# Values' bias moved into VectorE's evacuation of the shared block product, GpSimd's second bias pass dropped, and all places of the order replaced

## The chip, the core and the metric

The kernel runs on one core of a Trainium2 chip. The metric is the device time of one execution in microseconds (us); lower is better. TensorE is called PE below, its weight loads PEld, VectorE DVE, ScalarE ACT, GpSimd POOL and SyncE, which issues the DMAs, SP.

## The reference

64 independent graphs of 256 nodes with 256 features pass through two layers. All arithmetic is float32.

```
# layer 0, for each graph
q, k = x @ Wq + bq, x @ Wk + bk              # 8 heads of 32
attn = softmax(q k^T / sqrt(32))
out  = sum over r in 0..3 of (attn * (adj == r)) @ (x @ Wv[r] + bv[r])
x    = ln(x + out @ Wo + bo);  x = ln(x + gelu(x @ W1 + b1) @ W2 + b2)
# layer 1: two graph attentions, then a feed-forward
h = gat(gat(x, W1, a1), W2, a2)              # leaky relu, mask adj > 0, softmax
h = ln(x + h);  out = ln(h + relu(h @ w_ff1 + b_ff1) @ w_ff2 + b_ff2)
```

The part that is changed is `x @ Wv[r] + bv[r]`, the values of the four relations.

## The kernel before

**Tiling.** A graph fills 128 partitions twice: 256 nodes are two chunks (`C = 2`), 256 features two chunks (`KD = 2`). The values of a graph are a 256 x 256 by 256 x 1024 product, cut into 2 x 2 blocks. It is done in Strassen's manner with seven block products instead of eight: `v_product` (L504 to L511) makes product i, 128 x 512, in a PSUM buffer `v_ps`, and the sums that build the four blocks are made while the products are taken out of PSUM. Product 1 belongs to all four blocks: `v_first` (L522) copies it on ACT into block (0,0) of `v`, and `v_sum` (L518) adds the others on DVE, seven adds a graph, each from one block to the same or another one: block (1,0), for instance, starts as block (0,1) plus product 7. Then `v_bias` (L525) adds the bias rows on POOL: operation `vb1` adds the row of m = 1 to block (1,0), 512 columns, before (1,1) is made from it, and `vb0` adds the row of m = 0 to both blocks of m = 0, 1024 columns.

**Heads.** Of each graph's 2 x 4 heads, `scores` (L531) makes the scores of four heads by matmuls that use 32 rows of the array each, then come maximum, exponential, reciprocal and normalisation (`max`, `exp`, `rec`, `nrm`), a transposition by 32 x 32 squares on DVE with a write to DRAM and a read back (`eT`, `eW`, `eR`), a copy to PSUM (`ec`) and the products with the masks of the relations (`pm` on DVE, `pl` on POOL). `heads_out` (L580, matmuls L589) makes `po` by matmuls that use 32 columns of the array each. Operations `wo`, `st1` to `ln1` finish the attention; `a...` is the first feed-forward (`aT`, `aW`, `aR` transpose its input, `au` are its first products, `ad` its second), `ga...`, `z...`, `h1`, `h2` the graph attentions, `b...` the last feed-forward. The letter-and-number names are keys of `PLACES`.

**Order.** Nothing is scheduled by a compiler. `PLACES` (L28) gives each of a graph's operations a place; graph g's operations stand at `g * PERIOD + place` with `PERIOD = 60`, all are sorted (L781), and each engine carries out its own in that order, strictly one behind the other. The places are not times: a period takes 53.57 us on the chip. So in the steady state each engine repeats one cycle of operations, ordered by place modulo 60, that belong to about seven graphs. The four preparations of weights (`v_weights`, `ffn_weights` twice, `gat_weights`) and the loads of weights have places of their own (L68, L69) and are done once.

**Buffers.** All of PE's products apart from scores and the feed-forward's `po` bank share one PSUM pool of two buffers (`mm_tile`, L121). A product so waits until the reader of an earlier product, usually the last but one, is done.

Of the kernel before, what the change touches and what calls it, by code (L numbers as in the profile page):

```python
# [14 lines left out]
ALU = mybir.AluOpType  # L15
AX = mybir.AxisListType

P = 128
# [7 lines left out]

PERIOD = 60.0
PLACES = {  # L28
    "load": 51.115, "cast": 61.829, "xT": 85.66, "jT": 95.244, "mask0": 96.779, "qk0": 96.964,
    "qkc0": 97.949, "s0": 114.109, "mask1": 114.874, "max02": 120.516, "max01": 124.15, "exp02": 124.943,  # L30
    "rec02": 126.88, "nrm02": 128.516, "max00": 137.875, "max03": 138.248, "exp01": 142.049, "xS": 142.083,
    "eT02": 142.989, "exp00": 144.909, "rec01": 145.054, "qk1": 145.647, "exp03": 145.994, "eW02": 148.03,
    "rec00": 148.295, "qkc1": 149.435, "rec03": 149.477, "nrm01": 152.334, "mask2": 153.228, "vp1": 153.403,
    "nrm00": 154.4, "eT00": 155.05, "vc1": 155.594, "s1": 155.923, "nrm03": 158.066, "max10": 158.616,
    "max11": 159.127, "vp6": 159.308, "y": 159.875, "eR02": 161.643, "max13": 162.676, "mask3": 162.803,
    "exp10": 163.51, "exp13": 164.265, "va6": 164.378, "eW00": 164.574, "vp7": 165.766, "max12": 166.896,
    "vp2": 167.32, "eT03": 167.321, "exp12": 167.329, "va7": 168.263, "va1": 168.656, "pl02": 168.829,
    "eT01": 170.084, "vp5": 171.47, "vb1": 171.744, "va9": 173.956, "exp11": 174.017, "va5": 174.086,
    "eW01": 174.237, "vp4": 174.322, "rec11": 174.688, "rec10": 175.037, "ec02": 175.434, "nrm10": 175.847,
    "va4": 177.865, "nrm11": 178.881, "eW03": 179.53, "eT11": 180.637, "rec12": 181.004, "eR01": 181.498,  # L40
    "rec13": 182.146, "pm02": 182.221, "vp3": 182.341, "nrm13": 182.509, "eR00": 182.73, "mask4": 182.957,
    "ec01": 183.686, "va3": 183.974, "pl00": 184.596, "pm01": 184.674, "nrm12": 185.397, "eT13": 185.431,
    "eR03": 186.516, "ec00": 187.545, "eW11": 189.732, "eW13": 192.489, "pm00": 192.506, "eR11": 192.805,
    "pl03": 192.932, "pl01": 194.193, "ec03": 194.796, "vb0": 194.872, "pm03": 195.848, "eT10": 196.442,
    "eR13": 197.184, "eT12": 197.655, "po0": 199.032, "ec11": 199.429, "eW10": 200.338, "oT0": 203.052,
    "eW12": 203.488, "eR10": 203.542, "pm11": 203.833, "ec13": 205.99, "pm13": 207.559, "pl11": 208.544,
    "ec10": 209.569, "pm10": 210.783, "eR12": 211.055, "pl13": 211.531, "pl10": 212.738, "yb": 213.806,
    "ec12": 214.966, "pm12": 215.614, "pl12": 216.323, "po1": 224.021, "oT1": 226.193, "wo": 231.792,
    "ya": 235.114, "st1": 235.515, "rt1": 236.411, "nb1": 237.487, "ln1": 240.106, "aT": 241.237,
    "aW": 243.237, "aR": 244.635, "au0": 248.422, "au1": 248.889, "ax0": 249.225, "ax1": 250.028,  # L50
    "au2": 253.377, "aS1": 255.511, "ax2": 257.28, "au3": 257.297, "ag": 259.726, "ax3": 259.931,
    "ar": 263.256, "aS3": 265.084, "aS2": 265.188, "aS4": 266.76, "ad1": 267.736, "ad7": 268.061,
    "ad2": 269.978, "ad3": 270.34, "ad4": 270.945, "ae": 271.281, "ad5": 273.751, "ae1": 274.652,
    "ae7": 275.033, "ad6": 277.637, "ae5": 279.375, "ae6": 281.724, "st2": 283.997, "rt2": 284.29,
    "nb2": 285.905, "ln2": 291.498, "lg2": 293.887, "lb2": 294.79, "hT": 297.683, "hW": 300.513,
    "hR": 303.071, "ga0": 304.63, "gac0": 305.433, "ga1": 305.656, "gac1": 307.317, "ipA": 307.666,
    "zA": 307.902, "zmA": 307.921, "zxA": 308.379, "zeA": 312.657, "zdA": 315.675, "h10": 324.462,
    "h11": 325.343, "h1c0": 325.47, "h1c1": 325.478, "ipB": 327.18, "zB": 327.348, "zmB": 328.529,
    "zxB": 330.271, "zeB": 332.506, "zdB": 332.513, "h2": 335.643, "h2a": 335.996, "st3": 338.835,
    "rt3": 339.209, "nb3": 342.44, "ln3": 344.153, "bT": 344.795, "bW": 353.039, "bR": 353.733,  # L60
    "bu0": 358.326, "bu1": 358.559, "bx0": 358.988, "bu2": 361.425, "bx1": 361.898, "bx2": 361.904,
    "bu3": 362.148, "bx3": 363.223, "bS1": 363.277, "bd1": 364.353, "bg": 366.001, "bS2": 366.044,
    "br": 366.414, "bd5": 366.625, "bS4": 368.189, "bd6": 369.237, "bd2": 371.158, "bd3": 371.454,
    "be1": 372.63, "be5": 372.632, "bd4": 372.862, "bS3": 372.912, "be6": 374.175, "be": 375.364,
    "bd7": 377.598, "be7": 378.628, "st4": 383.514, "rt4": 389.43, "nb4": 404.438, "ln4": 418.122,
    "lg4": 419.704, "lb4": 422.082, "store": 423.961,
}
LOAD_PLACE, LOAD_STEP = 96.0, 3.0  # L68
V_PLACE, FFA_PLACE, GAT_PLACE, FFB_PLACE = 100.0, 240.0, 290.0, 300.0  # L69

# [11 lines left out]
def kernel(  # L84
# [12 lines left out]
    nc = tc.nc  # L97
    B, N, D = x.shape
    R = Wv.shape[0]
# [5 lines left out]
    C = N // P  # L105
# [35 lines left out]
    def weight(w, name, mixed=False):  # L141

        k, n = w.shape[0] // P, w.shape[1]
        t = const.tile([P, k, n], F32, name=name)
        if mixed:
            mixed_rows(t, w)
        else:
            loads.append((t, w.rearrange("(k p) n -> p k n", p=P)))
        return t
# [13 lines left out]
    def rowvec(v, n, name):  # L163
        t = const.tile([P, n], F32, name=name)
        loads.append((t, _row(v, n)))
        return t
# [21 lines left out]
    bv_r = const.tile([P, KD, R, P], F32, name="bv_r")  # L188
# [15 lines left out]
    wo, bo_r = weight(Wo, "wo"), rowvec(bo, D, "bo_r")  # L204
# [44 lines left out]
    def seven_weights(b, t):  # L249


        nc.vector.tensor_tensor(t[0], b[0][1], b[1][1], ALU.add)
        nc.vector.tensor_tensor(t[1], t[0], b[0][0], ALU.subtract)
        nc.vector.tensor_tensor(t[2], b[1][0], t[1], ALU.subtract)
        nc.vector.tensor_tensor(b[0][1], b[0][0], b[0][1], ALU.subtract)
        return {1: b[0][0], 2: b[1][0], 3: t[2], 4: b[1][1], 5: t[0], 6: t[1], 7: b[0][1]}

    def v_weights():
        wv_s.update(seven_weights([[wv[:, k, m].rearrange("p r n -> p (r n)") for m in range(KD)] for k in range(KD)],
                                  [wv_t[:, i] for i in range(3)]))  # L260

# [170 lines left out]
    class Graph:  # L432
# [87 lines left out]
            nc.vector.tensor_tensor(self.v_part(*to), self.v_part(*src), self.ps["v", i], ALU.add)  # L520

        def v_first(self):  # L522
            nc.scalar.copy(self.v_part(0, 0), self.ps["v", 1])

        def v_bias(self, m, jcs):  # L525
            v = self.v[m][:, jcs]
            row = bv_r[:, m].rearrange("p r n -> p (r n)")[:, None, :]
            nc.gpsimd.tensor_tensor(v.rearrange("p c r n -> p c (r n)"), v.rearrange("p c r n -> p c (r n)"),  # L528
                                    row.to_broadcast([P, len(range(C)[jcs]), R * P]), ALU.add)

        def scores(self, m):  # L531

# [154 lines left out]
        def operations(self):  # L687

            g, ops = self.g, {}
# [8 lines left out]
            for i in range(1, 8):  # L698
                ops[f"vp{i}"] = lambda i=i: self.v_product(i)

            ops["vc1"] = self.v_first
            for n, to, src, i in (("1", (0, 0), (0, 0), 2), ("6", (0, 1), (0, 0), 6), ("7", (1, 0), (0, 1), 7),
                                  ("5", (1, 1), (1, 0), 5), ("4", (1, 0), (1, 0), 4), ("9", (0, 1), (0, 1), 5),
                                  ("3", (0, 1), (0, 1), 3)):
                ops[f"va{n}"] = lambda to=to, src=src, i=i: self.v_sum(to, src, i)
            ops["vb1"] = lambda: self.v_bias(1, slice(0, 1))
            ops["vb0"] = lambda: self.v_bias(0, slice(0, C))
            for r in range(R + 1):
                ops[f"mask{r}"] = lambda r=r: self.mask(r)
            for m in range(KD):  # L710
# [59 lines left out]
    for place, f in (  # L770
            (V_PLACE, v_weights),
            (GAT_PLACE, gat_weights),
            (FFA_PLACE, lambda: ffn_weights(w1, b1_c, g1_c, be1_c, b2_r, be1_r, "ffa", w2, w2_t)),
            (FFB_PLACE, lambda: ffn_weights(f1, bf1_c, gl1_c, bl1_c, bf2_r, bl1_r, "ffb", f2, f2_t))):
        plan.append((place, len(PLACES), f))
    for g in range(B):
        ops = Graph(g).operations()
# [34 lines left out]
```

## Time and profile before

| what | value |
|---|---|
| median of 3 runs | 3575.66 us (3571.31 to 3575.95) |
| profiled execution, its own time | 3572.94 us |
| its span, first to last instruction | 3571.2 us |
| busy: PE, DVE, ACT, POOL | 3477.1, 2805.2, 2776.8, 3117.9 us |
| mean granted TensorE clock | 0.985 |
| HBM traffic over the span | 125 GB/s |

A busy share is an average over a fill (the first graphs), a long steady state and a drain (the last graphs). The profile's chain of waits follows the work that ended last back through the engines; a piece of PE in it with more microseconds than the same piece elsewhere holds a small pause. A list of waits names the engine that sat idle, the line it then ran, and who ended the wait.

### The profile page before, as it was taken

The numbers are of one execution on the slowest core, as the hardware profiler recorded it, in microseconds if no ns is written. First come the engines' busy times: TensorE is split into PE (matmuls) and PEld (weight loads), VectorE is DVE, ScalarE is ACT, GpSimd is POOL, SyncE is SP. The second block draws the span as 40 slices with busy tenths as digits, with TensorE's granted clock in tenths as the row PEclk, the third lists the DMA queues.
The fourth block names the chain that finished last, engine by engine and source line by source line (L and its number), as shares of the span: only waits on it lengthen the run. The fifth ranks groups of instructions, "written<-read, shape, count | busy, mean of one in ns | idle before, by whom it ended". The sixth has DMA issues, their size and how long they took to land.

```text
span 3571.2 us, 73514 instructions
## 1 busy us (share of the span) xinstructions
PE 3477.1 (97%) x25816; PEld 2704.2 (76%) x25816; DVE 2805.2 (79%) x4952; ACT 2776.8 (78%) x7107; POOL 3117.9 (87%) x3398
## 2 busy tenths in 40 slices
PE   6899999999999999999999999999999999999995
PEld 3677877877877877877877877877877877877875
DVE  5788888888888888788788888888788788788762
ACT  4677877877877877877877877877877877877863
POOL 4688988988988988988988988988988988988974
PEclk8899999999999999999999999999999999999997
DMA  7344444444444444444444444444444444444420
GB/s 198 112 126 127 131 135 127 131 135 127 131 135 127 131 135 128 131 135 126 132 135 125 133 135 125 133 135 122 135 136 122 135 136 122 135 136 123 132 86 27
DMA packets 809890, 457.97 MB, mean 128 GB/s; under 512 B 334256, under 2 KB 718896, under 8 KB 809520
## 3 DMA queue, kind: packets, MB, share of 16 engines
q1 hardware_dynamic: 809520, 453.27, 43.2%
q8 instruction: 203, 3.33, 0.4%
q14 instruction: 167, 1.37, 0.1%
HBM read 243.42 MB, written 201.33 MB: 125 GB/s over the span
## 4 chain that ended last, share of the span: by engine, by line
PE 95%; DMA 1%; DVE 1%; SPq 1%; POOL 1%; ACT 0%; issue 0%; POOLq 0%; ACTq 0%; DVEq 0%
PE po L589 13%; PE ffa_ps L387 12%; PE ffb_ps L387 12%; PE v_ps L511 11%; PE qk_ps L487 6%; PE ffa_po L422 6%; PE ffb_po L422 6%; PE ffa_pq L422 5%; PE ffb_pq L422 5%; PE s L537 4%; PE h_ps L664 3%; PE h_ps L678 3%; PE ga_wps L619 3%; PE wo_ps L609 3%; SPq L139 1%; PE ga_ips L631 0%
## 5 line engine op out<-in xcount | busy, mean ns | idle before, releaser
L572 DVE TENSOR_TENSOR pm<-rel,pe 128x1536 f32<-128x1536 uint8 x512 | 890.9, 1740 | 131.9 <-ACT pe L568 85.3
L577 POOL TENSOR_TENSOR pl<-rell,eT 128x512 f32<-128x512 bf16 x512 | 592.1, 1168 | 29.0 <-DMA eT<-eT_d 24.2
L550 ACT ACTIVATE e<-s,nmax 128x256 f32<-128x256 f32 x1024 | 474.7, 471 | 73.2 <-DVE eT_sq L306 63.6
L387 PE MATMUL ffb_ps<-ffb_T,f 128*128 128x256 f32 x2048 | 458.4, 382 | 24.0 <-DMA ffb_T<-ffb_T_d 23.8
L387 PE MATMUL ffa_ps<-ffa_T,w 128*128 128x256 f32 x2048 | 465.9, 381 | 8.3 <-DMA ffa_T<-ffa_T_d 8.2
L387 PEld LDWEIGHTS ffb_ps<-ffb_T,f 128*128 128x128 f32 x2048 | 392.6, 192 | 106.1 <-issue 39.4
L560 ACT ACTIVATE e<-e,rden 128x256 f32<-128x256 f32 x1024 | 462.4, 506 | 10.3 <-DVE rden L555 10.1
L479 POOL TENSOR_SCALAR rel<-adT 128x512 uint8<-128x512 bf16 x192 | 288.6, 1503 | 198.1 <-DVE pm L572 181.1
L387 PEld LDWEIGHTS ffa_ps<-ffa_T,w 128*128 128x128 f32 x2048 | 381.3, 191 | 57.8 <-ACT e L560 9.6
L520 DVE TENSOR_TENSOR v<-v,v_ps 128x512 f32<-128x512 f32 x448 | 296.0, 672 | 148.2 <-PE v_ps L511 142.5
L589 PE MATMUL po<-pm,v 128*32 128x256 f32 x6144 | 361.6, 384 | 15.7 <-POOL v L528 12.3
L306 DVE STREAM_TRANSPOSE eT_sq<-e 128x512 f32<-128x512 f32 x512 | 350.6, 694 | 3.3 <-ACT e L560 1.9
L395 ACT ACTIVATE ffb_h<-ffb_ps,bf_c 128x256 f32<-128x256 f32 x512 | 214.6, 470 | 160.6 <-PE ffb_ps L387 154.7
L542 DVE TENSOR_REDUCE nmax<-s 128x2 f32<-128x512 f32 x512 | 337.0, 669 | 0.0
L589 PEld LDWEIGHTS po<-pm,v 128*32 128x32 f32 x6144 | 188.7, 110 | 184.1 <-ACT e L560 46.2
L568 ACT COPY pe<-eT 128x512 f32<-128x512 f32 x512 | 303.3, 592 | 17.8 <-DMA eT<-eT_d 12.7
L528 POOL TENSOR_TENSOR v<-v,bv_r 128x512 f32<-128x512 f32 (+1 forms) x128 | 232.9, 1819 | 5.4 <-DVE v L520 1.1
L395 ACT ACTIVATE ffa_h<-ffa_ps,b_c 128x256 f32<-128x256 f32 x512 | 208.5, 475 | 5.5 <-PE ffa_ps L387 3.8
L496 ACT ACTIVATE qT<-qk_ps,bqs_c 128x256 f32<-128x256 f32 x128 | 60.7, 474 | 188.5 <-PE qk_ps L487 188.5
L550 ACT ACTIVATION_READ_ACCUMULATOR e<-s,nmax 128x1 f32 x1024 | 205.8, 201 | 0.0
L354 POOL TENSOR_TENSOR rs_x<-rs_x,nhalf 128x2 f32<-128x2 f32 x256 | 184.0, 719 | 21.3
L430 DVE TENSOR_TENSOR ffa_res<-ffa_po,ffa_res 128x256 f32<-128x256 f32 (+2 forms) x256 | 133.4, 521 | 69.9 <-PE ffa_po L422 65.6
(154 smaller groups left out, 8535.9 us busy)
## 6 DMA issues: line engine op xcount, KB each, us to landing
eT_d<-eT_sq SPq DMA_DIRECT2D x512, 256.0 KB, 2.1
eT<-eT_d SPq DMA_DIRECT2D x512, 256.0 KB, 3.2
xin<-in_x_dram SPq DMA_DIRECT2D x256, 64.0 KB, 2.5
adi<-in_adj_dram SPq DMA_DIRECT2D x64, 256.0 KB, 3.2
y<-in_x_dram SPq DMA_DIRECT2D x64, 256.0 KB, 3.1
ffa_T_d<-ffa_T_sq SPq DMA_DIRECT2D x64, 256.0 KB, 2.6
ffa_T<-ffa_T_d SPq DMA_DIRECT2D x64, 256.0 KB, 2.9
hT_d<-hT_sq SPq DMA_DIRECT2D x64, 256.0 KB, 2.1
```

Source lines behind the costliest of these rows:

```text
L306: nc.vector.transpose(self.sq.rearrange("p a c k y -> p (c k) a y"), src.rearrange("p c (k a x) -> p (c k) a x", k=KD, a=A))
L387: nc.tensor.matmul(p[:, f - f0, :], self.wa[:, k, f * P:(f + 1) * P], self.x.nodes(k), start=(k == 0), stop=(k == KD - 1))
L395: nc.scalar.activation(self.h[half][:, f1 + f, :], self.ps[f0][:, f, :], self.func, bias=self.ba[:, f0 + f:f0 + f + 1])
L422: nc.tensor.matmul(self.p[bank][:, k], a[:, f], seven[self.name[:3]][i][:, f], start=(f == 0), stop=(f == KF // 2 - 1))
L511: nc.tensor.matmul(self.ps["v", i], a, wv_s[i], start=True, stop=True)
L542: nc.vector.tensor_reduce(self.nmax[m, h], self.s4[m][h].rearrange("p (c n) -> p c n", c=C), AX.X, ALU.max, negate=True)
L550: nc.scalar.activation(e[:, ic, :], self.s4[m][h][:, ic * N:(ic + 1) * N], AF.Exp, bias=self.nmax[m, h][:, ic:ic + 1], accum_out=self.den[ ...
L560: nc.scalar.activation(e[:, ic, :], e[:, ic, :], AF.Copy, scale=self.rden[m, h][:, ic:ic + 1])
L568: nc.scalar.copy(self.pe[m, h], self.et[m, h].t.rearrange("p b c k y -> p (b c k y)"))
L572: nc.vector.tensor_tensor(self.pm[m, h], self.rel.rearrange("p r b c k y -> p r (b c k y)"), bc(self.pe[m, h], [P, R - 1, C * N]), ALU.mult)
L577: nc.gpsimd.tensor_tensor(self.pm_l[m, h], self.rel_l.rearrange("p b c k y -> p (b c k y)"), self.et[m, h].t.rearrange("p b c k y -> p (b ...
L589: nc.tensor.matmul(po[hp, :], self.v[m][:, jc, r, hp], w, start=(r == 0 and jc == 0), stop=(r == R - 1 and jc == C - 1))
```

## The change

Four edits, three of them in code and one in numbers.

1. `v_first` runs on DVE instead of ACT and adds the bias row of m = 0 while it takes product 1 out of PSUM. As product 1 goes into all four blocks, all four then hold that row.
2. `v_weights`, done once, first subtracts row 0 from row 1 in place, so that adding "row 1" to block (1,0) leaves that block with the true row 1; block (1,1) is made from it as before.
3. `vb0` is gone; `vb1` stays on POOL, once a graph, with 512 columns.
4. All places are new, and so are those of the loads and of the four preparations of weights.

```diff
-LOAD_PLACE, LOAD_STEP = 96.0, 3.0
-V_PLACE, FFA_PLACE, GAT_PLACE, FFB_PLACE = 100.0, 240.0, 290.0, 300.0
+LOAD_PLACE, LOAD_STEP = 164.4, 3.0
+V_PLACE, FFA_PLACE, GAT_PLACE, FFB_PLACE = 170.0, 322.0, 376.0, 380.0
...
+    def bias_row(m):
+        return bv_r[:, m].rearrange("p r n -> p (r n)")
+
     def v_weights():
+        nc.vector.tensor_tensor(bias_row(1), bias_row(1), bias_row(0), ALU.subtract)
...
         def v_first(self):
-            nc.scalar.copy(self.v_part(0, 0), self.ps["v", 1])
-
-        def v_bias(self, m, jcs):
-            v = self.v[m][:, jcs]
-            row = bv_r[:, m].rearrange("p r n -> p (r n)")[:, None, :]
-            nc.gpsimd.tensor_tensor(v.rearrange("p c r n -> p c (r n)"), v.rearrange("p c r n -> p c (r n)"),
-                                    row.to_broadcast([P, len(range(C)[jcs]), R * P]), ALU.add)
+            nc.vector.tensor_tensor(self.v_part(0, 0), self.ps["v", 1], bias_row(0), ALU.add)
+
+        def v_bias(self):
+
+            nc.gpsimd.tensor_tensor(self.v_part(1, 0), self.v_part(1, 0), bias_row(1), ALU.add)
...
-            ops["vb1"] = lambda: self.v_bias(1, slice(0, 1))
-            ops["vb0"] = lambda: self.v_bias(0, slice(0, C))
+            ops["vb1"] = self.v_bias
```

The places that are spoken of later, as they stand in the two tables (`load` to `store` is a graph's whole way):

| operation | before | after |
|---|---|---|
| load, store | 51.1, 424.0 | 98.4, 490.8 |
| qk1, s1, po0, po1 | 145.6, 155.9, 199.0, 224.0 | 185.3, 217.6, 278.3, 299.1 |
| wo, ln1, aT | 231.8, 240.1, 241.2 | 309.2, 318.6, 319.3 |
| h2, h2a, ln3, bT | 335.6, 336.0, 344.2, 344.8 | 412.8, 412.9, 419.7, 422.5 |
| va7, vc1 | 168.3, 155.6 | 242.6, 223.3 |

Modulo 60 this makes PE's cycle, written from `po0` on (runs of the feed-forwards' products are shortened to their letters):

```
before: po0 h10 h11 qk1 ipB ad vp1 ad h2 s1 qk0 ad vp6 po1 vp7 vp2 vp5 wo s0 vp4 bu vp3 bd ga bd ipA au bd au bd
after:  s1 po0 h10 h11 vp1 ad ipB ad qk0 ad vp6 ad h2 ad po1 vp7 vp2 qk1 vp5 s0 vp3 wo bu vp4 bd ga bd ipA bd au bd au
```

In the order of ACT's instructions, the loads of activation tables number 255 before and 129 after.

## The prediction

> **What bounds the kernel now.** First the page: busy times and the chain by engine.
>
> ```profile
> PE 3477.1 (97%) x25816; PEld 2704.2 (76%) x25816; DVE 2805.2 (79%) x4952; ACT 2776.8 (78%) x7107; POOL 3117.9 (87%) x3398
> PE 95%; DMA 1%; DVE 1%; SPq 1%; POOL 1%; ACT 0%; issue 0%; POOLq 0%; ACTq 0%; DVEq 0%
> ```
>
> Work taken off DVE, ACT or POOL is therefore worth nothing by itself; it counts where it makes PE wait less. So I split the span by stage (columns: us; busy PE, PEld, DVE, ACT, POOL; granted clock; DMA share; GB/s).
>
> ```profile
> 0.00:57.05 57.05, 26.20 (x86) 13.87 (x87) 27.76 (x47) 22.55 (x66) 23.21 (x27) 0.76 0.77 204
> 57.05:198.00 140.95, 122.09 (x886) 84.39 (x887) 103.86 (x173) 89.51 (x232) 89.83 (x93) 0.85 0.46 127
> 198.00:3400.00 3202.00, 3201.70 (x24015) 2501.21 (x24014) 2601.57 (x4590) 2586.65 (x6630) 2905.43 (x3161) 1.00 0.44 131
> 3400.00:3571.20 171.20, 127.11 (x833) 104.69 (x831) 72.01 (x146) 78.06 (x179) 99.44 (x119) 0.89 0.19 56
> ```
>
> PE idles 49.7 us in the fill (30.85 + 18.86), 44.1 us in the drain and 0.3 us in 3202 us between. About 60 periods are steady, 53.57 us each. To see pauses in a PE that never looks idle, I read one period of the chain (start, us, piece).
>
> ```profile
> 519.25 6.91 PE ffb_ps L387 x32
> 526.15 0.86 PE v_ps L511 x2
> ...
> 557.65 1.08 PE s L537 x16
> 558.72 1.92 PE qk_ps L487 x8
> 560.65 0.89 PE ffa_po L422 x8
> 561.54 0.86 PE v_ps L511 x2
> 562.40 3.59 PE po L589 x64
> 565.99 2.96 PE v_ps L511 x6
> 568.95 1.73 PE wo_ps L609 x8
> 570.68 1.07 PE s L537 x16
> 571.75 1.06 PE v_ps L511 x2
> ```
>
> A 256-column record takes 6.91 / 32 = 0.216 us, eight of them 1.73 (wo_ps), a 512-column record 0.43. Four records that share the array take one such slot. So `s` should take 4 x 0.216 = 0.86 and takes 1.08; what follows it takes 1.92 for 1.73 and 1.06 for 0.86. `po` should take 16 x 0.216 = 3.46 and takes 3.59; after it six v_ps take 2.96 for 2.57. Each `s` so costs 0.21 + 0.20, each `po` 0.13 + 0.20; the other 0.19 behind that `po` lies, by the matmuls' start times, between products 2 and 5: a wait for a PSUM buffer that DVE still reads. The qk_ps behind the first graph attention (1.81 for 1.73) waits 0.09 likewise. Per period: 2 x 0.41 + 2 x 0.33 = 1.49 us round `s` and `po`, 0.28 us of waits; the other 51.8 us are matmuls.
>
> **What the Trainium skill says.** "TensorEngine Tiling (Array Packing)", Key Properties: changing the tiling mode drains TensorE. The trace agrees: `s` (32-row tiles) and `po` (32-column tiles) are entered and left 8 times a period, 1.49 / 8 = 0.19 us each. "TensorE: Matmul & The Clock Gate", HAM oscillation: idling of more than about 3.4 us brings half clock. The trace agrees: 0.76 and 0.85 in the two stages with long idle gaps, 1.00 between. "GPSIMD Engine Reference", 3.1: a two-input add is about twice as slow on GpSimd as on VectorE; here 1272 against 672 ns:
>
> ```profile
> L520 DVE TENSOR_TENSOR v<-v,v_ps 128x512 f32<-128x512 f32 x448 | 296.0, 672 | 148.2 <-PE v_ps L511 142.5
> L528 POOL TENSOR_TENSOR v<-v,bv_r 128x1024 f32<-128x1024 f32 x64 | 151.4, 2366 | 0.0
> L528 POOL TENSOR_TENSOR v<-v,bv_r 128x512 f32<-128x512 f32 x64 | 81.4, 1272 | 5.4 <-DVE v L520 1.1
> L523 ACT COPY v<-v_ps 128x512 f32<-128x512 f32 x64 | 36.9, 577 | 0.0
> ```
>
> **The change part by part.** *The bias itself.* `vb0` leaves POOL: 2.37 us of a period in which POOL is busy 46 to 50 us. `v_first` leaves ACT (0.58 us) and costs DVE one more add from PSUM, 0.67 us on 44 us of busy time. All three hide under PE's 53.57 us: steady state 0. Without that cover DVE's add would cost 64 x 0.1 = 6 us over the copy. The subtraction in `v_weights` is one add of 0.7 us once, ahead of the first maxima on DVE, in the fill. By the list of waits, `vb0` is what the first `po` waited for:
>
> ```profile
> PE po L589 <- POOL v L528: 12.3, 1, 12.3
> PE ffa_ps L387 <- DMA ffa_T<-ffa_T_d: 8.0, 1, 8.0
> ```
>
> but `vb0` itself stood behind two `pl` on POOL that ended at 54.69, so at most 57.05 - 54.69 = 2.4 us go.
>
> *PE's new cycle.* Instructions and sizes of PE are the same. In it `s1` stands directly before `po0`: one run of tiled work instead of two. Seven mode changes are left instead of eight (full to row, row to column, column to full, and two each for `s0` and `po1`): -0.19 us a period. No neighbours of that kind stand in the trace, so both ends: free passage from row to column tiles would save 2 x 0.19 less nothing, about -0.33 (exit and entry both go); if the passage costs two drains, 0. I take one drain.
>
> *The waits.* Between products 2 and 5 now stands `qk1` (1.73 us), more than the 0.67 us of the DVE add that frees the buffer; the 0.19 us there should go, as should qk1's 0.09 behind `h11`, where `qk1` no longer stands. But a new order has new near misses. Lower end 0 left, upper end see the third rival; I keep half, 0.14 us: -0.14.
>
> *ACT's tables.* The instruction order holds 255 table loads before and 129 after, since all four `ax` now stand together. At the 1283 ns of the rows, 2 x 1.28 = 2.6 us of ACT's 43 us a period go; ACT is no bound, so 0, but its answers come sooner, which is why I trust the waits above to stay small.
>
> *Steady sum:* (-0.19 - 0.14) x 60 = -20 us.
>
> *Fill.* In the second wait shown, 8.0 us at 87 to 95 us, the first `aT` stood behind the preparation of the feed-forward's weights: ACT scaled weights (84.9 to 87.0) before `ln1` (to 88.1), DVE worked on weights before `aT` (89.66), and write and read ended at 95.1. Now `ln1` and `aT` (318.6, 319.3) stand before that preparation (322). With nb at 82.8, `ln1` ends at 83.9, `aT` at 84.6, the read at 90. Some 4.7 us of PE work (0.86 + 3.82) stand between `wo` (to 79.3) and `au`, so 5.6 us of gap remain of 8.0: -2.4. `qk1` and `s1` of the next graph are now done before the first `po`, 1.73 + 1.08 = 2.8 us of PE work in a gap of 12.3: -2.8. With the 2.4 of `vb0` that is -7.6, and the half clock behind each gap follows. Against it: the second graph's loads stand before the first mask transposition on SP (about 3.3 us of issues), and weights' loads and masks have moved too. I take -6, range -13 to +3.
>
> *Drain.* From `wo` to `store` the tail is 182 places instead of 192 and its chain through `h2a`, `st3`, `ln3`, `bT`, DRAM and back has the same instructions in the same order: 0, range -4 to +4. SP's issues are as many as before; `bW` and `bR` take about 5.5 us from `bT` and PE has 6.7 us of work after `qk1` before `bu`.
>
> *Total* 3572.94 - 20 - 6 = 3546.9 for the profiled execution. Its own time lies 2.7 us under the median of the runs, 3575.66, so against that 3575.66 - 26 = 3549.7: **3550 us**.
>
> **The rivals.** *One: nothing to be seen* (14 in 100). The passage from `s1` to `po0` costs as much as leaving and entering, and as much waiting comes back elsewhere as goes: 0 in the period, -3 in the fill, 3573 us. For it: PE is never idle, and waits in the period are only 0.28 us.
>
> *Two: everything comes* (12 in 100). Free passage (-0.33), no waits (-0.28), -12 in the fill: -0.61 x 60 - 12 = -49, 3527 us.
>
> *Three: slower, a new wait at `qk1`* (16 in 100). `qk1` needs the PSUM buffer of product 7, which `va7` frees; on DVE `va7` now stands behind `bT`, which waits for `ln3`, and so for `h2`. PE gives from the end of `h2` to `qk1`: two `ad` 0.89 + 0.98, `po1` 3.59, products 7 and 2 0.97 + 0.86, 7.3 us. The chain from `h2` to the end of `bT` took 5.3 us in the drain (3494.7 to 3500.0), `va7` adds 0.7: 6.0. `pm12` (1.74) may stand before `h2a`, and between `st3` and `bT` DVE has 3.4 us of other work (transposition 0.69, adds 0.69, 0.56 and 0.42, statistics 1.0) where the chain's POOL and ACT part leaves 2.8. Both together eat about the 1.3 us of slack. Queued behind `va7` are `va1`, `pm` and the next adds, which free the buffers for `vp5` and `wo`. Every us late costs 60 us; with the old waits gone too, it is slower from 0.19 + 0.28 + 0.1 (fill) = 0.57 us on. At 0.9: (-0.47 + 0.9) x 60 - 6 = +20, 3596 us.
>
> **How the numbers follow.** The forecast has 58 in 100; its own ends are (-0.12 - 0) x 60 + 2 = -5 and, as in rival two, nearly -45. What a measurement can tell from no change is 0.2%, 7 us: faster is under 3568.5, slower over 3582.8. Faster: 0.58, less 2, plus rival two and a fifth of rival one, 0.71. Slower: rival three and the drain and fill gone wrong, 0.17. Same: 0.12. The range of 8 in 10 takes the forecast, rival one and most of two: 3529 to 3577.
>
> **What would show it.** Right: a period of 53.2 us between the same pieces in the chain, `s` and `po` adjoining with one extra 0.2 us rather than two, 1.73 for the qk_ps behind v_ps, about 130 table loads, the first `po` before 57 us, no 8 us wait at the first ffa_ps. Wrong: PEld waits of qk_ps or v_ps on DVE of several tenths in each period; a period of 53.6 or more; gaps in the fill that are not in the old one.

## The result, and the profile after

| | before | after |
|---|---|---|
| median of the runs | 3575.14 us (3571.31 to 3575.95, 4 runs) | 3610.45 us (3609.5 to 3612.86, 4 runs) |
| profiled execution, its span | 3572.94, 3571.2 us | 3609.5, 3607.5 us |
| start to the first `ffb_ps` | 197.7 us | 203.3 us |
| the next 59 periods | 3161.6 us, typically 53.57 each | 3184.3 us, typically 53.91 each |
| 60th `ffb_ps` to the end | 211.9 us | 219.9 us |

The changed kernel is slower: ratio 1.0100, 95% interval 1.0087 to 1.0112. Forecast were 3550 us and a range of 3529 to 3577. The span grew by 36.3 us: 22.8 in the periods, 5.6 in the fill, 8.0 in the tail. (Cut at the starts of the first product of the last feed-forward, `ffb_ps`, so that the same piece ends each part.) A typical period grew by 0.345 us; 59 times that are 20.4 of the 22.8. The rest is a few longer periods, which I did not follow.

The page of the changed kernel, busy times and the chain by engine:

```profile
PE 3487.4 (97%) x25816; PEld 2732.6 (76%) x25816; DVE 2855.6 (79%) x5017; ACT 2585.6 (72%) x6917; POOL 2985.9 (83%) x3334
PE 77%; DVE 10%; ACT 8%; DMA 2%; POOL 1%; SPq 1%; issue 1%; ACTq 0%; POOLq 0%; DVEq 0%
```

What the change does to the engines is as foretold: ACT 191 us and POOL 132 us less, DVE 50 us more, PE's instructions the same; on the bias itself the rows of groups are these (the add that takes the copy's place has 690 ns, the POOL pass of 2366 ns is gone):

```profile
L527 DVE TENSOR_TENSOR v<-v_ps,bv_r 128x512 f32<-128x512 f32 x64 | 44.2, 690 | 0.0
L531 POOL TENSOR_TENSOR v<-v,bv_r 128x512 f32<-128x512 f32 x64 | 81.5, 1273 | 46.3 <-DVE rden L557 46.3
```

The page's second line is the news. Before, PE made up 95% of the chain; now 77%, with DVE and ACT in it for 18%: PE waits for them somewhere in each period. By stage (columns as in the prediction):

```profile
0.00:80.29 80.29, 36.95 (x190) 21.10 (x190) 42.98 (x69) 33.31 (x101) 29.55 (x36) 0.78 0.71 182
...
205.00:3420.00 3215.00, 3200.63 (x23948) 2515.75 (x23948) 2639.93 (x4642) 2399.70 (x6436) 2778.19 (x3099) 1.00 0.45 130
3420.00:3607.50 187.50, 137.05 (x886) 114.06 (x884) 76.08 (x150) 76.88 (x186) 101.28 (x120) 0.87 0.19 57
```

The first stage of this table ends inside the second `po`. The first `po`, with which the first stage of the table before ended, came at 57.05 us and now comes at 64.50:

```profile
64.50 3.61 PE L591 MATMUL po<-pm,v 128*32 128x256 f32 x48
```

In the steady stage PE idles 14.4 us in 3215, where it idled 0.3 in 3202. One period of the chain shows where (start, us, piece):

```profile
544.68 5.42 PE ffa_ps L391 x24
...
550.12 0.84 ACT ffa_h L399 x2
...
550.98 1.28 ACT L653
...
552.27 1.10 ACT ga_z L653 x4
...
553.40 0.17 DVE ga_rden L659
553.57 1.18 DVE nmax L544 x2
...
555.95 1.67 DVE pm L574
...
557.68 0.59 ACT pe L570
558.27 0.31 ACT gb_wh L672
...
558.63 0.43 PE gb_ips L633 x2
```

Read it as a relay that starts and ends on PE and lasts 8.5 us (550.1 to 558.63): the last up-product of the first feed-forward; its activations (`ffa_h`, operation ax3, 0.84); the load of the exponential's table (1.28, L653); the exponential of the first graph attention, zeA (1.10); on DVE its reciprocal, zdA (0.17), with maxima, a transposition and pm13 queued behind it; then on ACT the copy ec11 (`pe`), which needs the one `pe` buffer that pm13 frees, and behind ec11 the copy h1c1 (`gb_wh`); last ipB (`gb_ips`) on PE. PE's own work beside the relay, s1, po0, h1 and some products, is just too short. In the list of waits from 500 to 3400 us, the two links:

```profile
DVE ga_rden L659 <- ACT ga_z L653: 81.3, 53, 1.7
ACT pe L570 <- DVE pm L574: 79.2, 54, 1.7
```

DVE stands idle for zeA 1.5 us in every period, with the maxima queued behind the reciprocal; ACT stands idle for pm13 another 1.5, with h1c1 queued behind ec11.

I took the pauses of one period from the starts of the matmuls, as time from one start to the next above the 0.216 or 0.43 us of such a record. Where PE waits for a buffer, the pause has two parts in these traces: the wait before the first matmul, and then 0.10 us more between the first and the second (0.085 + 0.104 before qk1). The way out of a tiled run carries the same second part.

| pause of PE, us a period | before | after |
|---|---|---|
| round s1 and po0 (row and column tiles) | 0.74 | 0.55 |
| round s0 and po1 | 0.75 | 0.75 |
| product 2 to product 5 (before), to qk1 (after) | 0.19 | 0.19 |
| at the old place of qk1 | 0.09 | none |
| before ipB | none | 0.40 |
| before au1 (`ffa_ps` behind bd7) | none | 0.22 |

So 0.20 was gained, 0.09 went, and 0.62 came.

### The profile page after: what moved, and what is told of

Its sections match the earlier page's. It is cut to its first block, busy times and chain, and to the rows that moved or that the text cites. A ratio compares the mean times of both kernels' runs of the same rounds, so it can differ in the third digit from the quotient of the medians.

```text
span 3607.5 us, 73073 instructions
## 1 busy us (share of the span) xinstructions
PE 3487.4 (97%) x25816; PEld 2732.6 (76%) x25816; DVE 2855.6 (79%) x5017; ACT 2585.6 (72%) x6917; POOL 2985.9 (83%) x3334
## 4 chain that ended last, share of the span: by engine, by line
PE 77%; DVE 10%; ACT 8%; DMA 2%; POOL 1%; SPq 1%; issue 1%; ACTq 0%; POOLq 0%; DVEq 0%
PE ffa_ps L391 12%; PE ffb_ps L391 12%; PE v_ps L515 9%; PE qk_ps L491 6%; PE po L591 6%; PE ffb_po L426 6%; PE ffa_po L426 5%; PE ffb_pq L426 4%; PE ffa_pq L426 4%; DVE pm L574 3%; DVE nmax L544 3%; PE ga_wps L621 3%; PE h_ps L680 3%; PE wo_ps L611 3%; ACT L653 2%; PE s L539 2%
## 5 line engine op out<-in xcount | busy, mean ns | idle before, releaser
L391 PE MATMUL ffb_ps<-ffb_T,f 128*128 128x256 f32 x2048 | 460.6, 384 | 23.1 <-DMA ffb_T<-ffb_T_d 22.8
L391 PE MATMUL ffa_ps<-ffa_T,w 128*128 128x256 f32 x2048 | 473.9, 385 | 8.6 <-DMA ffa_T<-ffa_T_d 5.2
L562 ACT ACTIVATE e<-e,rden 128x256 f32<-128x256 f32 x1024 | 455.0, 503 | 0.1
L434 DVE TENSOR_TENSOR ffb_res<-ffb_po,ffb_res 128x256 f32<-128x256 f32 (+2 forms) x256 | 129.1, 504 | 129.9 <-POOL ffb_t L414 103.7
L368 ACT ACTIVATE ffa_res<-ffa_res,nb_x,rs_x 128x256 f32<-128x256 f32 x256 | 140.1, 598 | 114.1 <-POOL nb_x L363 110.0
L357 POOL TENSOR_SCALAR rs_x<-mv_x 128x2 f32<-128x2 f32 x256 | 56.6, 221 | 153.0 <-DVE mv_x L353 118.0
```

The costliest lines, as they stand in the source:

```text
L391: nc.tensor.matmul(p[:, f - f0, :], self.wa[:, k, f * P:(f + 1) * P], self.x.nodes(k), start=(k == 0), stop=(k == KD - 1))
L562: nc.scalar.activation(e[:, ic, :], e[:, ic, :], AF.Copy, scale=self.rden[m, h][:, ic:ic + 1])
```

## The experiments

All times are medians, all ratios against runs of the kernel before on the same chip (3573.59 to 3575.33 us by group). A theory stood for each pause: the relay for the 0.40, two steps on DVE ahead of the last feed-forward's sum `be`, which frees the buffer for au1, for the 0.22, bT ahead of va7 (the third rival's mechanism) for the 0.19.

**The three waits, one at a time, from the changed kernel.**

```diff
 e1:  "ec11": 282.871 -> 283.0       # behind h1c1 on ACT
 e2:  "pm13": 282.37  -> 278.6       # ahead of the maxima on DVE
 e3:  "bT":   422.521 -> 422.7       # behind va7 on DVE
 e4:  "zmA":  388.214 -> 389.7, "zxA": 388.489 -> 389.75   # behind be on DVE
 e5:  e2, e3 and e4 together
```

*e1.* 

> The changed kernel with one place moved (ec11 from 282.87 to 283.0), so that on ACT the copy h1c1 out of PSUM stands before ec11 instead of behind it. Theory (three waits): in each period PE waits 0.40 us before ipB for h1c1, which stands behind ec11, which waits for pm13 on DVE. The wait before ipB goes; ec11 and what hangs on it come as before. Period 53.91 to about 53.51 us, time about 60 x 0.40 = 24 us less than 3610, 3586 us. Rival (the bias add on DVE holds DVE up): the order of two copies on ACT has nothing to do with it, period stays 53.9, 3610 us. Rival (ACT's chain through the table load bounds the loop whatever its order): the wait moves to another PE instruction, period 53.8 or more, 3600 us or more.

Measured 3586.1 us, 1.0029 (1.0019 to 1.004), 24.4 less than the changed kernel; period 53.50; the pause before ipB is gone and no other has changed. One copy moved behind another takes 0.41 us from the period: h1c1 never needed pm13, it only stood behind a copy that did.

*e2.* 

> The changed kernel with one place moved (pm13 from 282.37 to 278.6), so that on DVE the masked product pm13 stands ahead of the four maxima and of the reciprocal that waits for the exponentials behind ACT's table load. Theory (three waits): the reciprocal's wait, 1.5 us of idle DVE a period, then delays no pm, pe is free early, ec11 and h1c1 come at once, and PE's 0.40 us before ipB go: period about 53.51 us, 3586 us, as in the run with the two copies turned round. Rival (bias add): 53.9, 3610 us. Rival (table load bounds): the table load and the exponentials stand where they were, so the wait stays, 53.9, 3610 us.

Measured 3803.45 us, 1.0638 (1.0622 to 1.0653): a miss, and a large one. The list of waits of this kernel tells why:

```profile
DVE pm L574 <- PE po L591: 235.9, 51, 5.0
```

pm13 needs one of the `pm` buffers that po0 is still reading. At its new place it stands just behind po0's start, and DVE waits 4.6 us (235.9 / 51) in each period for po0's end, with all maxima behind it. At the old place the maxima were the work that filled this time. I had looked at what pm13 reads, not at what it overwrites.

*e3.* 

> The changed kernel with one place moved (bT from 422.52 to 422.7), so that on DVE the add va7, which frees the PSUM buffer for qk1, stands before the transposition bT. Theory (three waits): PE's pause of 0.19 us round qk1 (0.085 of wait, 0.105 of restart) goes: period 53.91 to 53.72 us, 11 us less, 3599 us. Rival (the loop through the reciprocal and ec11 is the only bound, and PE only fills in its slack): period stays 53.9, 3610 us. Rival of the prediction (bT comes late and costs much): bT later by 0.7 us would make the last feed-forward wait, period 54.2 or more.

Measured 3641.6 us, 1.0186 (1.0171 to 1.0201): a miss, 31 us slower than the changed kernel. The pause of 0.19 before qk1 stays as it was, so bT ahead of va7 isn't its cause. In the timeline of the changed kernel DVE is idle for 0.9 us ahead of va7, waiting for product 7 itself: va7 starts 0.04 us behind product 7's end as the profile models it, takes 0.69, and qk1 starts 0.05 us behind va7's end. In the kernel before, product 5 followed va7 in the same way (0.04 and 0.05). The pause is this way through DVE, which is a little longer than the one product, product 2, that PE has to do beside it. What got worse is the other end: bT's way through DRAM is tight, in a typical period PE now pauses for 0.34 us at the first `ffb_ps`, and periods scatter from 54.0 to 56.9 us.

*e4.* 

> The changed kernel with two places moved (zmA, zxA from 388.21, 388.49 to 389.7, 389.75), so that on DVE the add be, which frees the PSUM buffer for au1, stands before the mask and the maximum of the first graph attention. Theory (three waits): PE's pause of 0.22 us before au1 (0.12 of wait, 0.10 of restart) goes: period 53.91 to 53.69 us, 13 us less, 3597 us. Rival (the loop through the reciprocal and ec11 is the only bound): au1 comes sooner, the loop begins with au3, so it shifts with it: the same gain; if instead nothing changes, 3610 us, PE's pause was slack of another wait.

Measured 3598.42 us, 1.0063 (1.0047 to 1.008), 12.0 less than the changed kernel; period 53.68. The pause before au1 is gone, as expected.

*e5.* 

> The changed kernel with pm13, bT, zmA and zxA moved at once (278.6, 422.7, 389.7, 389.75). Theory (three waits): all three pauses go, period 53.91 - 0.40 - 0.19 - 0.22 = 53.10 us, which is the 51.8 us of matmuls and 1.3 us of mode changes; 60 x 0.81 = 49 us less than 3610, 3561 us, below the kernel before by 14 us, though the fill and the tail still cost 14 us more. Rival (the pauses cover one another): period 53.3 to 53.5, about 3580 us. Rival (bias add on DVE): no gain, 3610 us.

Measured 3827.48 us, 1.0709 (1.069 to 1.0727). It holds e2's and e3's mistakes and tells nothing further.

**Code and places apart.** e6 is the kernel before with the new code for the bias and its old places, without vb0; e7 has the new places and the old code.

```diff
 e6, in the kernel before (with the subtraction in v_weights):
-            nc.scalar.copy(self.v_part(0, 0), self.ps["v", 1])
+            nc.vector.tensor_tensor(self.v_part(0, 0), self.ps["v", 1], bias_row(0), ALU.add)
-            ops["vb0"] = lambda: self.v_bias(0, slice(0, C))
 e7, in the changed kernel (without the subtraction):
-            nc.vector.tensor_tensor(self.v_part(0, 0), self.ps["v", 1], bias_row(0), ALU.add)
+            nc.scalar.copy(self.v_part(0, 0), self.ps["v", 1])
+            ops["vb0"] = lambda: self.v_bias(0, slice(0, C))      # place 272.0
```

*e6.* 

> The kernel before with the bias edit alone: v_first adds row 0 on DVE, row 0 is subtracted from row 1 once, vb0 is gone, all other places are those of before. Theory (places): the three engines concerned are hidden under PE, so the period stays 53.57 us; in the fill the first po waited for vb0, up to 2.4 us go: 3573 to 3576 us. Rival (bias add on DVE holds DVE up): the period grows towards 53.9, 3595 us or more.

Measured 3585.76 us, 1.0033 (1.002 to 1.0047): a miss, 11 us slower. The period is 53.75, 0.185 longer, and it lies where va7 frees the buffer for product 5: the six `v_ps` behind po1 lost 0.30 and now lose 0.48. Product 7 on PE and va7 on DVE, in the kernel before:

```profile
565.92 1.13 PE L511 MATMUL v_ps<-wv,xs 128*128 128x512 f32 x2
567.08 0.69 DVE L520 TENSOR_TENSOR v<-v,v_ps 128x512 f32<-128x512 f32 x1 [0.28 <-PE v_ps L511]
```

The same in e6:

```profile
567.53 1.12 PE L515 MATMUL v_ps<-wv,xs 128*128 128x512 f32 x2
568.92 1.31 DVE L524 TENSOR_TENSOR v<-v,v_ps 128x512 f32<-128x512 f32 x2
```

Before, DVE had been idle for 0.28 us when product 7 came, and va7 began 0.03 us behind its end (567.05). In e6 the added instruction, 0.65 us long, has used up this idle time, and va7 begins 0.27 us behind product 7's end (568.65). DVE is busy for only 44 of 53.6 us, but in the 9 us between the new add and va7 it has no pause to give, and PE waits for va7. In the fill the first `po` does start 2.6 us sooner (54.41 us instead of 57.05), as vb0's 2.4 us promised, but the start of the first `ffb_ps` hardly moved (197.7 to 198.1): the gain was lost again on the way.

*e7.* 

> The changed kernel's places with the bias as it was before: v_first a copy on ACT, vb0 on POOL (placed at 272.0, behind pl01), no subtraction. Theory (places): all that was lost is in the places, so the period stays at 53.9 us and the time at 3605 to 3615 us. Rival (bias edit): the time comes back to about 3580 us.

Measured 3621.44 us, 1.0135 (1.012 to 1.015), 11.0 more than the changed kernel; a typical period is 54.13. With the old code a further pause of 0.22 us stands before qk0, which needs the buffer that product 1's copy on ACT frees. The pause before ipB is 0.40 with the old code too, so the add on DVE is not its cause.

**The fill.**

```diff
 e8:
-LOAD_PLACE, LOAD_STEP = 164.4, 3.0
+LOAD_PLACE, LOAD_STEP = 205.0, 3.0
```

The trace of the changed kernel up to 210 us has these two waits that the kernel before does not have at this length:

```profile
DVE eT_sq L310 <- DMA eT_d<-eT_sq: 9.1, 2, 8.2
PEld qk_ps L491 <- DVE v L524: 11.6, 4, 9.3
```

The transposed squares `eT_sq` have three buffers, and a buffer is free once its write to DRAM has landed. SP issues these writes, and from place 164.4 on it first issues 20 loads of weights (19 by the expectation below) and those of the third graph, so that the first write is issued at 36.3 us (26.1 in e8). DVE waits for one write 8.2 us, the sums of the values stand behind it, and qk waits for the sums.

*e8.* 

> The changed kernel with the 49 loads of the later weights placed from 205.0 on instead of 164.4, so that on SP most of them stand behind the first graph's transpositions. Theory (fill): the first graph's eT transpositions use three buffers and wait for writes that SP issues behind 19 weight loads and the third graph's load; with some 13 loads fewer ahead of the first write (0.6 us each) the first po starts about 8 us sooner than 80.3 us, of which some 5 to 8 us reach the end: 3602 to 3605 us, period unchanged at 53.91. Rival (the fill is bound by PE's and DVE's own order): under 2 us, 3610 us.

Measured 3600.13 us, 1.0077 (1.006 to 1.0094), 10.3 less than the changed kernel. The period is the same, 53.91. The 80.3 us of the expectation lie inside the second `po`; the first starts at 57.16 us instead of 64.50, and the first `ffb_ps` at 196.6 instead of 203.3. So the loads' place was the fill's whole loss (5.6 us) and a little more. The tail of the profiled execution is 3.4 us shorter besides, 216.5 us, at the same order and almost the same idle time of PE (50.4 for 50.7 us), but at a granted clock of 0.91 instead of 0.89; that this comes from the loads is not shown. One wait of the fill stays:

```profile
PE s L539 <- ACT e L552: 20.4, 4, 8.9
```

The longest of the four is that of the second graph's s1, which stands right ahead of the first `po` now and waits until ACT's exponentials have read the earlier scores.

**Together.** e9 is the changed kernel with e1, e4 and e8. e10 is e9 with `"s0": 188.717 -> 184.6`, which puts s0 between product 2 and qk1. e11 is e10 with bd7 between s1 and po0 (`"bd7": 450.217 -> 457.6`, be7, st4 and rt4 behind it).

*e9.* 

> The changed kernel with three edits of places together: the copy ec11 behind h1c1, the two masks zmA and zxA behind be, and the loads of weights from place 205 on. Taken one by one they saved 24.4, 12.0 and 10.3 us of 3610.4. Theory (the change itself is sound, its loss is three new waits that the new places make, each in a place of its own): the savings add, 3564 us, period 53.28 us, faster than the kernel before (3575). Rival (the waits share one slack: where one goes another engine is late next, as with the wait at product 5 that only passed to qk1): less than half of it adds, 3585 us or more and a period of 53.6 or more.

Measured 3563.44 us (3561.31 to 3564.97), 0.997 (0.9959 to 0.9982); period 53.28. The three savings add up (3563.8 by the sum; that it fits within 1 us is closer than the runs, which scatter by 4 us, allow to claim), and the kernel is faster than the one before. PE makes up 93% of the chain on its page, where it made up 77% in the changed kernel. Its tail, 221.3 us, is still 9 us longer than before.

*e10.* 

> As the mended kernel (e9), and s0 stands between product 2 and qk1 instead of behind product 5. Theory: qk1 waits 0.19 us for the buffer that va7 frees because nothing but product 2 stands between; 1.08 us of s0 in that place cover it, the wait goes and is not passed on: period 53.09, 3552 us. Rival: the wait passes to whatever asks for the next buffer (product 5 behind qk1, on va2), or s0 itself waits for ACT's exponentials: period 53.28 or more, 3564 us or more.

Measured 3598.03 us, 1.0069 (1.0056 to 1.0081): the rival was right. The wait before qk1 is gone, and in its place:

```profile
PEld wo_ps L611 <- DVE v L524: 54.5, 54, 1.0
PEld v_ps L515 <- ACT kT L502: 48.5, 54, 0.9
```

s0 needs none of the two shared buffers, and so gives the readers 1.08 us wherever it stands. Behind product 5 it had given them to ACT's copies of qk1 and to product 5's sum; without it product 3 and `wo` lose 0.79 us, four times what qk1 got (0.19).

*e11.* 

> As e10, and the eighth product bd7 of the last feed-forward stands between s1 and po0, so that the two tiled runs are apart as before the change; its sum be7 and the statistics follow it. Theory (one change of tiling mode costs 0.19 to 0.20 us): period 0.20 longer than e10's, 53.29, 12 us more, 3564 us. Rival (the passage from rows to columns costs as much as leaving and entering): the period stays within 0.05 of e10's. bd7 four microseconds later may free a wait too, which the pauses of the period would show separately.

Measured 3627.99 us, 1.0151 (1.0137 to 1.0165); period 54.35, 0.47 longer than e10's. The chain of e11 over the place:

```profile
1846.11 3.72 PE ffa_ps L391 x16
1849.83 1.07 PE s L539 x16
1850.91 1.09 PE ffb_po L426 x8
```

`ffb_po` takes 1.09 for 0.89: 0.195 us for leaving the row tiles and entering the column tiles, where e10 has the passage from one to the other alone. That is the price of one change, which was asked for. The other 0.27 us lies ahead of it: `ffa_ps` takes 3.72 for 3.46. By the list of waits DVE now waits 3.2 us a period for bd7; which of the steps behind it holds the up-products back I did not follow.

**What stayed open after these.** e12 is e9 with the old code for the bias (as in e7). e13 is e9 with another order in the last two graphs alone:

```diff
+        last = {"zmA": 388.209, "zxA": 388.489, "zeA": 390.4, "zdA": 390.6} if g >= B - 2 else {}
-        plan += [(g * PERIOD + t, i, ops[n]) for i, (n, t) in enumerate(PLACES.items())]
+        plan += [(g * PERIOD + last.get(n, t), i, ops[n]) for i, (n, t) in enumerate(PLACES.items())]
```

*e12.* 

> The mended kernel (e9) with the old code for the bias: product 1 is copied on ACT, and vb0 is back on POOL behind the two pl that end the heads of m = 0. It tells what the bias edit is worth by itself in places that hold no other new wait. Theory (a copy on ACT stands behind the copies h1c1 and ec11 in the two-buffer cycle, as in the after places, so that qk0 waits 0.2 us for it, where an add on DVE is in time): period 53.50, 13 us more than e9, 3577 us, so about the time of the kernel before. Rival (the edit's 11 us in the after places were the same stretch as the wait before ipB, which the mended places took away): within 0.05 of e9's period, 3561 to 3567 us.

Measured 3588.61 us, 1.0037 (1.0024 to 1.0049), 25 more than e9; a typical period is 53.62, 0.345 longer. The theory was right in kind and too small in size (0.22 expected). The wait is named: 0.28 us of the weight load (14.6 / 53), of which PE itself lost 0.25, with 0.10 behind it. That is the whole difference, so vb0 on POOL costs nothing in the period:

```profile
PEld qk_ps L490 <- ACT v L526: 14.6, 53, 0.4
```

*e13.* 

> The mended kernel (e9), and in the last two graphs alone the exponential and division of the first graph attention (zeA, zdA) stand ahead of the next graph's activations ax0 to ax3 instead of behind ax3, and zmA and zxA ahead of be again. Theory (in the drain no s1 and po0 are left to cover the way from ax3 through the table load, zeA and zdA to h1, and the 4.1 us idle gap of PE before h1 at 3466 us is this way): the gap goes, the tail from the 60th ffb_ps to the end falls from 221.3 to 217 to 218 us, 3560 us, the period as in e9. Rival (the way to the last feed-forwards through ln3, bT and DRAM sets the end whatever stands before): PE idles there instead, the tail stays within 1 us of 221.3.

Measured 3561.17 us (3559.5 to 3562.76), 0.9964 (0.995 to 0.9977). The tail falls from 221.3 to 215.0 us in the profiled execution. PE's gap of 4.1 us before h1 is gone (1.0 us before an up-product stands in its place), and the one in the last graph falls from 3.7 to 2.0. In all PE idles 48.2 us in the tail instead of 51.6 (50.4 to 51.7 in the changed kernel, e1, e4, e8 and e9): these 3.4 us are what the order gives, and they are near the 4 expected. In the other 3 us PE did the same work faster, as the half clock was granted for 42 us of the tail instead of 48. How much of that follows from the order is not shown: e8's tail was 3.4 us shorter than the changed kernel's at the same order. The way to the last feed-forwards did not take the gain back. Against e9 the whole time is not told apart (the ranges overlap).

## Why the prediction was wrong

By its own steps:

- **What bounds the kernel** was right: PE's period, with PE 97% busy before and after, and fractions of a microsecond that count 60 times.
- **"Seven mode changes are left instead of eight"**, priced at -0.19 us a period, was right: 0.20 by the pauses of the two profiles, 0.195 by e11. The Trainium skill, "TensorEngine Tiling (Array Packing)", Key Properties, says that a change of mode drains TensorE; these runs add that a direct passage from row to column tiles costs one change, not two and not none.
- **The waits, "-0.14", is the step that failed**: they came to +0.53 (0.40 + 0.22 - 0.09). At 60 periods that is 40 us between forecast and result, and it turns the sign. It failed in three places. First, "the 0.19 us there should go", as `qk1` stands between products 2 and 5 now: the buffer that va7 frees goes to the next product that asks, whatever it is. With qk1 between, qk1 itself asked, and waited the same 0.19. The third rival says itself that `qk1` needs the buffer of product 7; the forecast counted it as work that covers the wait for this buffer. e10, the one other order tried, moved the waiting and made it longer. Second, the relay from ax3 to ipB: I followed single waits of PE, and left out zdA's reciprocal in DVE's queue and ec11 in ACT's, which tie the two together (e1). Third, `be` behind two steps of the graph attention on DVE (e4).
- **"Its answers come sooner, which is why I trust the waits above to stay small"** was no argument. ACT has 191 us less to do, but the load that stands between ax3 and zeA lies in the relay. A count of loads says nothing on whether one of them is waited for. The Trainium skill, "ScalarE: Activation LUTs", What ACT_TABLE_LOAD costs, gives 1283 ns for the load and about 1380 ns of draining; the trace has the 1.28 us, but between ax3's end at 550.96 us and the exponential's start at 552.27 there is no more than the load and 0.03 us. The measurement decides here: 1.3 us a switch.
- **"Steady state 0" for the bias edit** was wrong in both directions. Its worth is set by the places: +11 us in the old ones (e6), -11 in the new (e7), -25 in the mended (e12). "All three hide under PE's 53.57 us" looks at sums of busy time, and DVE's 44 of 53.6 us say nothing about the one sum that PE waits for. The text even priced the lost cover, as 0.1 us a period over the copy; the unit that matters was the whole add in DVE's queue, 0.65 us, against the 0.28 us of idle time that DVE had ahead of va7. Neither half of the change gains alone: the new code in the old places costs 11 us, and the old code in the mended places is 13 us slower than the kernel before.
- **Fill, -6 with a range of -13 to +3**: it was +5.6. That "weights' loads and masks have moved too" was named as a risk and not followed: by e8 the loads cost 6.7 us. But with the loads mended the fill is only 1.1 us shorter than before, where three gains were to sum to 7.6. Moving aT ahead of the weights' preparation did shorten the gap before the first `ffa_ps`, to 5.0 us from 8.0 (6.1 in e8). The first `po` did not gain: even in e8 it starts at 57.16 us, as before (57.05), although vb0 is gone. `s1` of the second graph was counted as 1.08 us of work to fill the gap; it has a wait of its own, 8.9 us, and PE takes `po0` only behind it.
- **Drain, 0 ("the same instructions in the same order")**: it was +8.0, of which 6.7 are idle time of PE (50.7 us instead of 44.0). The order in one graph is the same; between neighbouring graphs it is not. zeA stands behind the next graph's ax3, and in the drain nothing covers that (e13 takes 3.4 us of idle time of PE back). Why the rest of the tail is longer stays open.
- **The third rival** had the sign, and not the mechanism: e3 rules out bT ahead of va7 for the wait at qk1. Its remark that bT's way is tight is borne out by e3's scatter.
- **Sums.** Three are off by little and decide nothing: free passage at "2 x 0.19" saves 0.38 and not 0.33; a read at 90 us and PE work up to 84.0 (79.3 + 4.7) leave 6.0 us of gap and not 5.6; and PE's work from `qk1` to `bu` comes to 6.5 us with `qk1` in it, not 6.7 behind it.

What the change is worth is so: with its two new waits and the loads mended by four numbers (e9) it gives 0.3% (0.18 to 0.41%), from 0.20 us of one mode change and 0.09 of a wait: 15 us over 59 periods and 2 in the fill, less 9 in the tail. The forecast of 3550 had the right kinds of gain, and missed 47 us in two waits and the loads (24.4, 12.0 and 10.3) and the tail. Not settled is whether the 0.19 before qk1 can be had at all: s0 in that place was tried, other orders were not.

## What to carry to other kernels

When all places of a hand-made order are new, follow each engine's queue, not each wait: for every wait of the bounding engine write down the whole queue ahead of the instruction that ends it, on every engine the relay passes, and what each of these instructions overwrites as well as what it reads. A wait on a shared buffer goes to the next customer unless its reader ends earlier or something that needs no buffer stands before it. An edit priced at nothing because its engine has idle time must be looked up at the one place where the bound engine waits for that engine.

## What the runs showed of the hardware

Behind a wait of PE for a PSUM buffer, another 0.10 us were lost between the first matmul and the second: 0.085 + 0.104 before qk1 and 0.12 + 0.10 before au1 in the changed kernel (e4 gives both parts of the latter back), 0.246 + 0.104 before qk0 in e12, 0.345 + 0.104 before `wo` in e10. The pause of 0.09 at the old place of qk1 was such a second part alone. Before ipB, whose matmuls take 0.11 us each, the parts were 0.355 and 0.05. The way out of a tiled run carries 0.10 as well. As an estimate from these figures that no run tested, two waits of 0.1 us would cost 0.4 us and one of 0.2 us would cost 0.3.

A direct passage from row tiles to column tiles saved 0.20 us over leaving the one and entering the other with other work between (0.55 instead of 0.74 round s1 and po0; 0.195 by e11).

A switch of ACT's tables took 1.31 us from the end of one activation to the start of the next: in the 106 switches of the changed kernel's steady stage, 0.02 us, the load of 1.28, and 0.01.
